# A conditioned residual kernel: convolution results of chunks 1 to 3 kept in DRAM, 29 adapter weights fetched ahead, D's row as an input

## The chip, the cores and the metric

The kernel runs on one core of a Trainium2 chip. The metric is the device time of one execution in microseconds (us); lower is better. Before the change it was run three times; the median is 2402.39 us (2400.78 to 2402.60). The trace that is shown comes from one more execution, taken by the hardware profiler.

The names of the engines are those of the profile: PE is TensorE (PEld its weight load), DVE is VectorE, ACT is ScalarE, POOL is GpSimd, and SP is SyncE, which here only issues DMAs. "SPq" in the trace is the queue of SP. Every engine carries out its own list of instructions in the order of the list.

## The reference

The input x has 32 sequences of 64 rows and 1024 columns, all float32. Four layers are added to it one after the other, each with indices per sequence:

```python
x = x + L0(x, log_dt, C, log_A_real, A_imag, D, length)   # long convolution
x = x + einsum('bsi,boi->bso', x, w1[ids1])               # first adapter, 1024x1024 per sequence
x = x + einsum('bij,bkj->bik', x, w2[ids2])               # second adapter
x = x + L3(x, W_gate, W_up, W_down, low-rank parts)       # gated layer, 2752 hidden columns

def L0(u, ...):
    K = 2 * real(einsum('hn,hnl->hl', Ct, exp(P)))        # one filter of 1024 taps per row h
    y = causal_convolution(u, K) + u * D[:, None]
    return y * (arange(1024) < length[:, None])[:, None, :]
```

Since D multiplies u itself, it may be added to the first tap of the filter of its row.

## The kernel before

The 32 sequences are four chunks of eight (`NCK`, `BC`). A chunk is a tile x of 128 partitions x 8 x 512 float32 (2 MB): the 1024 columns are 8 tiles (`KT`) of 128 partitions, and the 512 columns of a tile are 8 sequences x 64 rows. Only two such tiles have a permanent place (`xpool`, two buffers).

**Convolution** (`convolution`, lines 600 to 883). It runs over the rows h of all sequences at once. `kernels(g)` builds the filters of a group of 4 or 8 rows from sines, cosines and exponentials (POOL for the arguments, line 698, then DVE and ACT), multiplies them on PE into `pk` (line 804) and writes them through ACT's queue to DRAM (`kp`, line 816). D enters as a product of its own: POOL writes D's values of the group into an otherwise zero tile `dk` (line 778), which PE multiplies by a selecting matrix (line 795, 32x256). `convolve` (line 823) then takes four rows: it loads the input `uf` (512 KB) and, from `kp`, for two rows at a time, the shifted filters `hk` (1 MB, line 833), runs 16 products for each pair (line 845), masks the result on DVE into `tmp`, and POOL adds `tmp` to the x tiles of all four chunks, four instructions of 128x256 (line 861). All four x tiles therefore have to be on chip: two in `xpool` and two in `x2pool`. 16 calls of `convolve` cover the 64 rows.

**Adapters** (`adapter`, line 163; `adapters`, line 199). For one sequence and one of the two adapters eight weight tiles of 512 KB are loaded by SP, chosen by an index which SP reads from `ids_sb`, and PE multiplies them (line 184, 64 products). DVE transposes the result and adds it to x (lines 195 and 197). A weight goes into one of nine places `early`, or, once these are used up, into one of the nine buffers of `wpool`, which all weights of the kernel share. All 16 calls of chunk 0 (128 weight tiles, 64 MB) run right after the convolution, and `early` is released after them.

**Gated layer** (`ffn`, line 458), once for each chunk: `rest` (line 401), products of 128x512 with three weights `wr`, and in it `expand` (line 297) with the gathered rows `bgu` of the low-rank part; then ten blocks `gated(c, m)` (line 346), each of which starts with `expand(b_rows(c, m), ...)`: POOL gathers 128 rows by an indirect DMA (line 221) into the single buffer of `bgu`, and PE multiplies them (line 305) before the big products `pf` (line 361). After each half of a block `between` is called, which interleaves the adapters of the next chunk (`other`). `prepare` computes the low-rank columns of the next chunk. POOL also issues the loads of the columns `raw_g`, `raw_u`, `raw_d` (line 249); the buffer of `raw` is single, so that the next set waits for ACT's copy (line 254).

**x of chunks 2 and 3**. In the first `between` of chunk 0, POOL writes both tiles to DRAM (`park`, line 126), and at the first `between` of chunks 1 and 2 SP loads one of them back (line 485) into the buffer of `xpool` that the chunk before has left, after its output has been written (line 589, ACT's queue).

**Order.** PE's list is the order of the program text (`manual_schedule(engines={PE})`). The lists of the other engines are drawn up by a scheduler from its own estimate of times; `issue_after` gives it an earliest place. The DMAs that SP and ACT issue use eight completion semaphores in turn; a DMA waits for the one that used its semaphore before.

Of the kernel before, what the change touches and what calls it, by code (L numbers as in the profile page):

```python
# [8 lines left out]
F32 = mybir.dt.float32  # L9
I32 = mybir.dt.int32  # L10
AF = mybir.ActivationFunctionType
ALU = mybir.AluOpType
# [17 lines left out]
EARLY = 9  # L30
# [35 lines left out]
def kernel(  # L66
# [44 lines left out]
    def x_tile(pool, c, tag):  # L111
        return pool.tile([P, KT, TC], F32, tag=tag, name=f"x{c}")

    ctx.enter_context(tc.manual_schedule(engines={PE}))
    xs = [x_tile(xpool, c, "x") for c in range(2)]

    right = ExitStack()
    x2pool = right.enter_context(tc.tile_pool(name="x2pool", bufs=1, side="right"))
    first = right.enter_context(ExitStack())
    epool = first.enter_context(tc.tile_pool(name="epool", bufs=1, side="right"))  # L120
    late = [x_tile(x2pool, c, f"x{c}") for c in range(2, NCK)]
    early = [epool.tile([P, L], F32, tag=f"e{i}", name=f"early{i}") for i in range(EARLY)]
    blocks = convolution(tc, cst, consts, xt, xf, ssm, lens, xs + late, ps_tile)
    parked = []

    def park():
        for c, x_c in enumerate(late, 2):
            d = dpool.tile([P, KT, TC], F32, tag=f"xd{c}", name=f"xd{c}")
            nc.gpsimd.dma_start(d, x_c)
            parked.append(d)  # L130

    ids_sb = cpool.tile([1, 3 * B], I32, tag="ids", name="ids_sb")
    nc.sync.dma_start(ids_sb, ids)

# [25 lines left out]
    loads = []  # L160
    ypool = ctx.enter_context(tc.tile_pool(name="ypool", bufs=2, reuse_waits="tile"))

    def adapter(w, layer, b):
        c, lo = b // BC, (b % BC) * H
        with ExitStack() as after:
            if len(loads) > 3:

                after.enter_context(tc.issue_after(loads[-4]))
            e = nc.values_load(
                ids_sb[0:1, layer * B + b : layer * B + b + 1],  # L170
                engines=[SP],
                min_val=0,
                max_val=NE - 1,
            )
        acc = ps_tile(f"pa{layer}_{b}")
        for kt in range(KT):
            name = f"wa{layer}_{b}_{kt}"
            wt = early.pop(0) if early else wpool.tile([P, L], F32, tag="w", name=name)
            load = nc.sync.dma_start(
                wt, w[bass.ds(e, 1), kt].rearrange("e p f -> p (e f)")  # L180
            )
            for s in range(2):
                for i in range(4):
                    nc.tensor.matmul(  # L184
                        acc[i * S : (i + 1) * S, s * 256 : (s + 1) * 256],
                        xs[c][:, kt, lo + s * S : lo + (s + 1) * S],
                        wt[:, i * 256 : (i + 1) * 256],

                        start=(kt == 0 and s == 0),
                        stop=(kt == KT - 1),  # L190
                        skip_group_check=True,
                    )
        loads.append(load.ins)
        y = ypool.tile([P, 512], F32, tag="y", name=f"y{layer}_{b}")
        nc.vector.transpose(y, acc)  # L195
        cols = xs[c][:, :, lo : lo + H].rearrange("p k (s t) -> p k s t", t=S)
        nc.vector.tensor_add(cols, cols, y.rearrange("p (s k t) -> p k s t", s=2, t=S))

    def adapters(c):


        for b in range(c * BC, (c + 1) * BC + 1):
            if b < (c + 1) * BC:
                yield adapter(w1, 0, b)
            if b > c * BC:
                yield adapter(w2, 1, b - 1)

    with tc.issue_after(blocks[5]):

        pieces = adapters(0)  # L210
        for _ in range(3):
            next(pieces)
    for _ in pieces:
        pass
# [18 lines left out]
    apools = []  # L233
# [112 lines left out]
    def gated(c, m, xb, between):  # L346
# [47 lines left out]
        act = apools[0].tile([P, 2, TC], F32, tag="act", name=f"act_{c}_{m}")  # L394
# [63 lines left out]
    def ffn(c, xb, others):  # L458
# [6 lines left out]
        def other(share, of=2 * FM * AT_GATED + (2 * KH - 3) * AT_DOWN):  # L465
            due[0] += share * NPIECE
            while due[1] * of < due[0]:
                next(others, None)
                due[1] += 1

        def between(i):
            if i == 0 and c == 0:
                with tc.issue_after(cols[-1]):
                    park()
                right.close()
                apools.append(
                    ctx.enter_context(
                        tc.tile_pool(
                            name="apool", bufs=MB, side="right", reuse_waits="tile"
                        )  # L480
                    )
                )
            if i == 0 and c and c + 1 < NCK:
                x_n = x_tile(xpool, c + 1, "x")
                nc.sync.dma_start(x_n, parked[c - 1])
                xs.append(x_n)
            other(AT_GATED)
# [3 lines left out]
        for block, (m0, m1) in enumerate(BLOCKS):  # L491
# [7 lines left out]
            if last:  # L499


                wl = gpool.tile([P, 2, 2, L // 2], F32, tag="wl", name=f"wl_{c}", bufs=1)
                for t in (0, 1):
                    wl_t = wl[:, t].rearrange("p i f -> p (i f)")
                    gather(wl_t[FIRST], bd, rows_half[FIRST, c, t : t + 1])
                    nc.sync.dma_start(wl_t[SECOND], wd_rest)
                nc.vector.tensor_sub(wl[:, 1, 0], wl[:, 1, 0], wl[:, 1, 1])
            else:
                ins += [rest1, rest2.rearrange("p i t -> p (i t)")]

            ab = []
            for i, act in enumerate(acts):
                t3 = apools[0].tile([P, 4, TH], F32, tag="actd", name=f"actd_{c}_{m0 + i}")
                q = [act[:, h, t * TH : (t + 1) * TH] for h in (0, 1) for t in (0, 1)]
                ab.append(moving(*q, *(t3[:, j] for j in range(4))))
# [84 lines left out]
def convolution(tc, cst, consts, xt, xf, ssm, lens, xs, ps_tile):  # L600
# [9 lines left out]
    with ExitStack() as ctx:  # L610
# [12 lines left out]
        for c in range(NCK):  # L623
            nc.sync.dma_start(xs[c], xt[:, c])
# [141 lines left out]
        zero = s1.tile([HG, P], F32, tag="zero", name="zero")  # L766
        nc.vector.memset(zero, 0.0)


        dk = s1.tile([P, HG, LQ], F32, tag="dk", name="dk")  # L770
        nc.gpsimd.memset(dk, 0.0)

        def kernels(g):
# [3 lines left out]
            r = powers(g, y, s1, "r")  # L777
            nc.gpsimd.tensor_copy(dk[0:1, :n, 0], dskip[0:1, h0 : h0 + n])
# [15 lines left out]
            ps = ps_tile(f"pk{g}")[:LQ, : n * LQ]  # L794
            nc.tensor.matmul(
                ps,
                cst[:, CO_SEL : CO_SEL + LQ],
                dk[:, :n].rearrange("p h l -> p (h l)"),
                start=True,
                stop=False,  # L800
                skip_group_check=True,
            )
            for i in range(n):
                nc.tensor.matmul(
                    ps[:, i * LQ : (i + 1) * LQ],
                    gt[:, i, :],
                    et[:, i, :],
                    start=False,
                    stop=True,
                    skip_group_check=True,  # L810
                )
            ks = s2.tile([LQ, HG, LQ], F32, tag="ks", name=f"ks{g}")
            nc.scalar.copy(ks[:, :n].rearrange("a h b -> a (h b)"), ps)
            kp = dram.tile([n, KROW], F32, tag=f"kp{g}", name=f"kp{g}")
            nc.scalar.dma_start(kp[:, :P], zero[:n])
# [5 lines left out]
        loads = []  # L821

        def convolve(kp, row, ha):

            uf = s3.tile([P, 4, KT, B], F32, tag="uf", name=f"uf{ha}", bufs=2)
            nc.sync.dma_start(uf, xf[:, ha : ha + 4])
            tmp = s2.tile([P, 4, KT * B], F32, tag="tmp", name=f"tmp{ha}")
            for i in range(0, 4, 2):
                hk = s3.tile([P, 2, L], F32, tag="hk", name=f"hk{ha + i}")

                for j in range(0, 2, 1 if ha == 0 else 2):
                    n = 1 if ha == 0 else 2
                    load = nc.sync.dma_start(
                        hk[:, j : j + n],
                        bass.AP(
                            tensor=kp.tensor,
                            offset=kp[row + i + j : row + i + j + 1, 1:2].offset,
                            ap=[[1, P], [KROW, n], [1, L]],
                        ),
                    )  # L840
                loads.append(load.ins)
# [16 lines left out]
            tv = tmp.rearrange("p i (k b) -> p k b i", b=B)  # L858
            for c in range(NCK):
                xv = xs[c].rearrange("p k (b h) -> p k b h", h=H)[:, :, :, ha : ha + 4]  # L860
                nc.gpsimd.tensor_tensor(xv, xv, tv[:, :, c * BC : (c + 1) * BC, :], ALU.add)
# [15 lines left out]
        for g, n in enumerate(GROUPS):  # L877
            h0 = sum(GROUPS[:g])
            for i in range(0, n, 4):
                convolve(ready[g], i, h0 + i)  # L880
                if i == 0 and g + 2 < len(GROUPS):
                    ready.append(kernels(g + 2))
        return loads
# [19 lines left out]
def _layouts(np, v):  # L903
# [8 lines left out]
    def states(a):  # L912
# [10 lines left out]
            np.broadcast_to(v["L0_cond_D"], (P, H)),  # L923
# [4 lines left out]
    def adapters(w):  # L928
        w = w.reshape(NE, KT, 4, S, KT, P)
        return w.transpose(0, 4, 5, 2, 1, 3).reshape(NE, KT, P, L)  # L930
# [104 lines left out]
```

## Time and profile before

| | us |
|---|---|
| median of three runs | 2402.39 |
| the profiled execution | 2400.47 |
| its span, first to last instruction | 2398.80 |
| PE busy | 2324.7 (97% of the span) |
| POOL busy | 206.8 (9%) |
| DMA, mean over the span | 209 GB/s |

Three stretches can be told apart. From 0 to some 196 us the filters are built and the convolution runs. From 197 to 360 us PE runs the adapters of chunk 0 and waits again and again for a weight; the DMA engines are full there. From then on the gated layers follow, in which PE is busy nearly all the time: of the stretch from 440 to 2000 us the table of stages shows every microsecond as busy. A wait that is added to PE's list there has nothing beside it that could hide it, and where PE is busy all the time a wait of another engine costs nothing.

In the lines of the timeline the first number is the start in us, the second the length, then engine, line of the kernel, operation, output and inputs, the shape, the number of instructions that are merged, and in brackets how long the engine was idle before and what ended that.

### The profile page before, as it was taken

The numbers are of one execution on the slowest core, as the hardware profiler recorded it, in microseconds if no ns is written. First come the engines' busy times: TensorE is split into PE (matmuls) and PEld (weight loads), VectorE is DVE, ScalarE is ACT, GpSimd is POOL, SyncE is SP. The second block draws the span as 40 slices with busy tenths as digits, with TensorE's granted clock in tenths as the row PEclk, the third lists the DMA queues.
The fourth block names the chain that finished last, engine by engine and source line by source line (L and its number), as shares of the span: only waits on it lengthen the run. The fifth ranks groups of instructions, "written<-read, shape, count | busy, mean of one in ns | idle before, by whom it ended". The sixth has DMA issues, their size and how long they took to land.

```text
span 2398.8 us, 46172 instructions
## 1 busy us (share of the span) xinstructions
PE 2324.7 (97%) x19154; PEld 1837.2 (77%) x19154; DVE 1087.4 (45%) x2067; ACT 310.8 (13%) x605; POOL 206.8 (9%) x301
## 2 busy tenths in 40 slices
PE   4998888999999999999999999999999999999999
PEld 3995335787787786788787786788787787888888
DVE  7511113454344543554344533554444544554653
ACT  4200002110011101110011101110011101210210
POOL 3533001000000020000000020000000020000000
PEclk9999999999999999999999999999999999999999
DMA  7889997656656646656756646655756543223311
GB/s 274 286 290 369 408 408 273 217 211 210 228 202 226 226 149 213 228 202 211 244 189 244 208 148 215 242 189 201 269 182 248 185 158 115 82 84 108 99 55 62
DMA packets 163139, 501.21 MB, mean 209 GB/s; under 512 B 20018, under 2 KB 54130, under 8 KB 161906
## 3 DMA queue, kind: packets, MB, share of 16 engines
q1 hardware_dynamic: 146434, 461.78, 55.2%
q0 software_dynamic: 9568, 27.80, 3.6%
q10 hardware_dynamic: 6928, 8.69, 1.0%
q8 instruction: 151, 2.47, 0.4%
q14 instruction: 58, 0.48, 0.1%
HBM read 485.31 MB, written 12.88 MB: 208 GB/s over the span
## 4 chain that ended last, share of the span: by engine, by line
PE 90%; DMA 7%; DVE 1%; ACT 1%; issue 0%; POOL 0%; SPq 0%; ACTq 0%; DVEq 0%; POOLq 0%
PE pf L361 41%; PE po L558 20%; PE pa L184 15%; DMA wa<-in_w 6%; PE pc L845 5%; PE pr L421 3%; PE po L553 2%; PE pe L305 2%; PE pl_d L277 1%; PE pl_u L277 0%; PE pl_g L277 0%; DVE br L645 0%; DMA ln<-in_lens 0%; DMA hk<-kp 0%; DMA kp<-ks 0%
## 5 line engine op out<-in xcount | busy, mean ns | idle before, releaser
L361 PE MATMUL pf<-xd,wf 128*128 128x256 f32 x2560 | 607.2, 381 | 0.0
L361 PEld LDWEIGHTS pf<-xd,wf 128*128 128x128 f32 x2560 | 481.6, 190 | 75.4 <-issue 7.4
L184 PE MATMUL pa<-wa,x 128*32 128x256 f32 x8048 | 468.8, 382 | 28.0 <-DMA wa<-in_w 26.4
L361 PE MATMUL pf<-xd,s 128*128 128x256 f32 x1920 | 453.7, 379 | 2.3 <-ACT c L377 2.3
L184 PEld LDWEIGHTS pa<-wa,x 128*32 128x32 f32 x8048 | 248.2, 110 | 241.2 <-DMA wa<-in_w 70.5
L361 PEld LDWEIGHTS pf<-xd,s 128*128 128x128 f32 x1920 | 364.7, 190 | 52.3 <-ACT c L377 2.7
L845 PE MATMUL pc<-uf,hk 128*128 128x256 f32 (+7 forms) x1024 | 151.8, 311 | 11.8 <-DMA hk<-kp 11.8
L221 POOL DMA_INDIRECT bgu<-in_bgu,rows x44 | 45.5, 1033 | 1354.8 <-PE pe L305 1305.7
L558 PE MATMUL po<-act,wd 128*128 128x256 f32 x640 | 161.7, 383 | 0.0
L845 PEld LDWEIGHTS pc<-uf,hk 128*128 128x128 f32 x1024 | 147.3, 194 | 15.9 <-issue 12.0
L558 PE MATMUL po<-actd,wd 128*128 128x256 f32 x640 | 159.0, 379 | 0.0
L558 PE MATMUL po<-actd,s 128*128 128x256 f32 x640 | 159.0, 379 | 0.0
L386 DVE TENSOR_TENSOR c<-pf,u 128x256 f32<-128x256 f32 x80 | 34.0, 425 | 242.3 <-PE pf L361 242.3
L558 PEld LDWEIGHTS po<-act,wd 128*128 128x128 f32 x640 | 119.4, 190 | 22.9 <-issue 6.3
L558 PEld LDWEIGHTS po<-actd,wd 128*128 128x128 f32 x640 | 121.6, 190 | 16.5
L558 PEld LDWEIGHTS po<-actd,s 128*128 128x128 f32 x640 | 121.6, 190 | 16.5
L315 ACT COPY lt<-pe 128x512 f32<-128x512 f32 x160 | 82.2, 599 | 307.5 <-PE pe L305 216.1
L195 DVE STREAM_TRANSPOSE y<-pa 128x512 f32<-128x512 f32 x64 | 45.5, 711 | 142.0 <-PE pa L184 142.0
L390 DVE TENSOR_TENSOR c<-c,lt 128x1024 f32<-128x1024 f32 x80 | 98.0, 1225 | 6.4
L333 DVE TENSOR_TENSOR s<-wf 128x512 f32<-128x512 f32 x80 | 54.7, 684 | 89.3 <-DMA wf<-in_wg 43.3
L333 DVE TENSOR_TENSOR s<-wd 128x384 f32<-128x384 f32 x64 | 31.2, 487 | 129.7 <-PE po L558 95.8
L421 PE MATMUL pr<-x,wr 128*128 128x512 f32 x192 | 84.2, 595 | 0.0
(166 smaller groups left out, 1816.6 us busy)
## 6 DMA issues: line engine op xcount, KB each, us to landing
wa<-in_w SPq DMA_DIRECT2D x503, 512.0 KB
wf<-in_wg SPq DMA_DIRECT2D x80, 512.0 KB
wf<-in_wu SPq DMA_DIRECT2D x80, 512.0 KB
wd<-in_wd SPq DMA_DIRECT2D x96, 384.0 KB
hk<-kp SPq DMA_DIRECT2D x30, 1024.0 KB
x<-in_xt SPq DMA_DIRECT2D x4, 2048.0 KB
uf<-in_xf SPq DMA_DIRECT2D x16, 512.0 KB
wd<-in_wd SPq DMA_DIRECT2D x32, 256.0 KB
```

What stands on the lines that cost most here:

```text
L184: nc.tensor.matmul(acc[i * S : (i + 1) * S, s * 256 : (s + 1) * 256], xs[c][:, kt, lo + s * S : lo + (s + 1) * S], wt[:, i * 256 : (i + 1) ...
L195: nc.vector.transpose(y, acc)
L221: nc.gpsimd.indirect_dma_start(out=t, out_offset=None, in_=table, in_offset=bass.IndirectOffsetOnAxis(ap=at_, axis=0),)
L305: nc.tensor.matmul(ps[:, at_ * 2 * H : (at_ + 1) * 2 * H], bt[pair(j), g], tms[table][pair(j)], start=(g == 0), stop=True, skip_group_chec ...
L315: nc.scalar.copy(lt[:, :n, 2 * H * j : 2 * H * (j + 1)], ps[:, : n * 2 * H].rearrange("p (i t) -> p i t", i=n),)
L333: nc.vector.tensor_add(s1, a21, a22)
L361: nc.tensor.matmul(ps, ws[j][:, kt, :], xb[j][:, kt, :], start=start and kt == 0, stop=kt == KH - 1, skip_group_check=True,)
L390: nc.vector.tensor_add(cf, cf, lt[:, g].rearrange("p i t -> p (i t)"))
L421: nc.tensor.matmul(ps, wt[:, kt, :], xs[c][:, kt, :], start=(kt == 0), stop=(kt == KT - 1),)
L553: nc.tensor.matmul(pss[j], w, a, start=False, stop=False, skip_group_check=True)
L558: nc.tensor.matmul(pss[j], ws[j][:, i, :], ab[m - m0][j], start=(m == m0 and home[j] % 2 == 0), stop=(m == m1 - 1), skip_group_check=True,)
L845: nc.tensor.matmul(ps[:, j, d * B :], hk[:, j, d * P : (d + 1) * P], uf[:, i + j, : KT - d, :].rearrange("p k b -> p (k b)"), start=(d == ...
```

## The change

Six things change together.

1. **Chunks 1 to 3 wait in DRAM.** `convolve` adds `tmp` only to chunk 0 (one POOL instruction instead of four). The parts of the other three chunks are copied by POOL into a tile `co` (128x768) and written by POOL's queue to a DRAM tile `cd`: 16 writes of 384 KB, in pieces of 1 KB.
2. **x of chunks 1 to 3 is loaded when it is needed.** `bring(c + 1, part)` is called in the first two `between` of chunks 0 to 2. It loads x from the input (2 MB), loads the four quarters of the convolution's result (`cv`, 512 KB each, into buffers of `wpool`), and POOL adds them: 16 instructions of 128x256 for a chunk. `park` and the loads from it go.
3. **More weights ahead.** `early` has 16 places of its own and four more in the x tile which chunk 1 will use; with the nine of `wpool` 29 weights of the adapters can be fetched during the convolution. `fetch` asks for 14 in the first `convolve`, ahead of the first `hk`, and for one in each of the other 15.
4. **D's row.** D comes in as a row with zeros below it, and one product of 8 columns (4 in the small groups) adds it to the first column of each row of `pk`; `dk`, its copies on POOL and the product of 256 columns go. The zeros ahead of the filters are written once for all groups instead of nine times, and the arguments `r` of the filters get two buffers instead of one.
5. **The interleaving.** The first two `between` of a chunk bring x and do no adapter; the other calls share the 16 adapters, so that they come a little more densely.
6. **SP's list.** `ids_sb` is loaded first of all, since the early weights need the indices. The loads of `wd_rest` get an earliest place, after the loads of chunk 0's adapters.

The core of the diff:

```diff
-EARLY = 9
+EARLY = 16
+FIRST_LOADS = 14
+PLACES = EARLY + 4 + 9
+HA = 4
...
+    early += [
+        place[:, i : i + L // TC].rearrange("p k t -> p (k t)")
+        for i in range(0, KT, L // TC)
+    ]
+    cd = dpool.tile([NCK - 1, P, H // HA, HA * KT * BC], F32, tag="cd", name="cd")
...
+    def fetch(ha):
+        for _ in range(FIRST_LOADS if ha == 0 else 1):
+            if len(ahead) < PLACES:
+                ahead.append(next(stream))
+
+    convolution(tc, cst, consts, xt, xf, ssm, lens, xs[0], cd, ps_tile, fetch)
+
+    def bring(c, part):
+        if part == 0:
+            xs.append(x_tile(c))
+            with tc.issue_after(loads[2 * BC - 1]):
+                nc.sync.dma_start(xs[c], xt[:, c])
+        n = H // HA // 4
+        for q in (2 * part, 2 * part + 1):
+            t = wpool.tile([P, n, HA * KT * BC], F32, tag="w", name=f"cv{c}_{q}")
+            nc.sync.dma_start(t, cd[c - 1][:, q * n : (q + 1) * n])
+            for g in range(n):
+                h = (q * n + g) * HA
+                xv = xs[c].rearrange("p k (b h) -> p k b h", h=H)[:, :, :, h : h + HA]
+                tv = t[:, g].rearrange("p (i k b) -> p k b i", k=KT, b=BC)
+                nc.gpsimd.tensor_tensor(xv, xv, tv, ALU.add)
...
         def between(i):
-            if i == 0 and c == 0:
-                with tc.issue_after(cols[-1]):
-                    park()
...
-            if i == 0 and c and c + 1 < NCK:
-                x_n = x_tile(xpool, c + 1, "x")
-                nc.sync.dma_start(x_n, parked[c - 1])
-                xs.append(x_n)
-            other(AT_GATED)
+            if i < 2:
+                if c + 1 < NCK:
+                    bring(c + 1, i)
+            else:
+                other(AT_GATED)
...
-            r = powers(g, y, s1, "r")
-            nc.gpsimd.tensor_copy(dk[0:1, :n, 0], dskip[0:1, h0 : h0 + n])
+            r = powers(g, y, s2, "r")
...
             nc.tensor.matmul(
-                ps,
+                ps[:, :, 0],
                 cst[:, CO_SEL : CO_SEL + LQ],
-                dk[:, :n].rearrange("p h l -> p (h l)"),
-                start=True,
-                stop=False,
+                dskip[:, h0 : h0 + n],
+                start=False,
+                stop=True,
                 skip_group_check=True,
             )
...
             uf = s3.tile([P, HA, KT, B], F32, tag="uf", name=f"uf{ha}", bufs=2)
             nc.sync.dma_start(uf, xf[:, ha : ha + HA])
+            fetch(ha)
...
-            tv = tmp.rearrange("p i (k b) -> p k b i", b=B)
-            for c in range(NCK):
-                xv = xs[c].rearrange("p k (b h) -> p k b h", h=H)[:, :, :, ha : ha + 4]
-                nc.gpsimd.tensor_tensor(xv, xv, tv[:, :, c * BC : (c + 1) * BC, :], ALU.add)
+            xv = x0.rearrange("p k (b h) -> p k b h", h=H)[:, :, :, ha : ha + HA]
+            tv = tmp.rearrange("p i (k b) -> p k b i", b=B)[:, :, :BC, :]
+            nc.gpsimd.tensor_tensor(xv, xv, tv, ALU.add)
+            co = s1.tile([P, NCK - 1, HA * KT, BC], F32, tag="co", name=f"co{ha}")
+            tv = tmp.rearrange("p i (k c b) -> p c (i k) b", k=KT, b=BC)[:, 1:]
+            nc.gpsimd.tensor_copy(co, tv)
+            nc.gpsimd.dma_start(
+                cd.rearrange("c p g e -> p c g e")[:, :, ha // HA],
+                co.rearrange("p c i b -> p c (i b)"),
+            )
```

The lists of the changed kernel's instructions, engine by engine, are known before it runs. Where they matter for the prediction, it says what stands in them.

## The prediction

> **What bounds the kernel now.** I read the page first: PE is busy for 97% of the span and the chain of waits is 90% PE, 7% DMA, with one DMA group that matters, the adapter weights.
>
> ```profile
> PE 90%; DMA 7%; DVE 1%; ACT 1%; issue 0%; POOL 0%; SPq 0%; ACTq 0%; DVEq 0%; POOLq 0%
> ```
>
> Then the table of stages, to see where these 7% lie (columns: window, length, busy us and instructions of each engine, granted clock, DMA share, GB/s):
>
> ```profile
> 120.00:180.00 60.00, 60.00 (x438) 58.13 (x437) 8.68 (x13) 0.72 (x2) 21.71 (x28) 1.00 0.85 290
> 240.00:300.00 60.00, 49.61 (x748) 19.87 (x744) 8.45 (x12) 1.99 (x2) 0.00 (x0) 1.00 1.03 408
> 420.00:480.00 60.00, 60.00 (x542) 47.34 (x545) 28.97 (x49) 8.59 (x19) 2.21 (x2) 1.00 0.61 216
> ```
>
> The convolution (first row) is bound by PE, with the DMA at 290 GB/s; the adapters of chunk 0 (second row) by the DMA at its limit of 408 GB/s; the gated layers (third row) by PE alone. In the first and third kind of stage a stall of PE is paid in full.
>
> Third, the timelines of PE, POOL and SP at the start of chunk 1, the place where the change puts new work:
>
> ```profile
> 905.86 0.52 POOL L433 MEMSET rest<- 64x512 f32 x1 [7.34 <-DVE x L581]
> 906.67 0.94 POOL L221 DMA_INDIRECT wl<-in_bd,rows_half  x1 [0.28 <-issue]
> 907.92 0.92 POOL L221 DMA_INDIRECT wl<-in_bd,rows_half  x1 [0.30 <-issue]
> 921.83 0.97 POOL L221 DMA_INDIRECT bgu<-in_bgu,rows  x1 [13.00 <-PE pe_rest L305]
> 930.00 0.96 POOL L221 DMA_INDIRECT bgu<-in_bgu,rows  x1 [7.20 <-PE pe L305]
> ```
>
> ```profile
> 905.85 1.16 SPq L506 DMA_DIRECT2D wl<-in_wd_rest  x2
> 917.30 0.34 SPq L485 DMA_DIRECT2D x<-xd  x1
> ```
>
> ```profile
> 921.38 7.13 PE L421 MATMUL pr<-x,wr 128*128 128x512 f32 x16
> 928.45 0.73 PE L305 MATMUL pe<-tm_g,bgu 32*128 32x128 f32 x16
> ```
>
> The gather of `bgu` for the first block is issued at 921.83, as soon as PE has released its buffer, and PE uses it at 928.45 without idling: 6.6 us of cover, no more. x of the next chunk is issued by SP only at 917.30, because it waits for the output of chunk 0. Before, nothing waits for that x for a long time. Last, the price of POOL's addition:
>
> ```profile
> 187.19 3.24 POOL L861 TENSOR_TENSOR x<-x,tmp 128x256 f32<-128x256 f32 x4 [5.96 <-DVE tmp L637]
> ```
>
> 0.81 us each undisturbed; the mean of 60 between 60 and 200 us is 0.89.
>
> **What the Trainium skill says.** "TensorE: Matmul & The Clock Gate", in its opening table, gives GpSimd a queue of strict order; the trace agrees (the gathers above run one by one in list order). "GPSIMD Engine Reference", section 3.1, measures about 2.6 cycles per element for a two-input addition; at 256 elements and 1.2 GHz that is an estimate of 0.55 us plus dispatch, below the trace's 0.81, which I use. "TensorE: Matmul & The Clock Gate", part 1, says that PE falls to half clock after an idle window of some 3.4 us and needs about as long to recover; the trace agrees: after the idle time from 54.7 to 59.1 us the clock of the window from 59 to 66 is 0.76, a loss of 0.24 x 7 = 1.7 us. "DMA: Bandwidth & Descriptors", section "Issuing engines are not separate DMA queues", says that queues share the same engines, so the new writes on POOL's queue take bandwidth from `hk`; no stage of this trace has both at full load.
>
> **The change, part by part.**
>
> *Adapters of chunk 0: -22.8 us.* Before, from the first product (197.27) to the last transpose (360.05), 162.8 us. PE takes a tile in 0.44 us (17 tiles in 7.55), the DMA delivers one in 1.28 (ten-odd pieces of 10.1 us for eight). After, 29 tiles lie ready, but SP's list continues with the 30th only when the first `wpool` tile, the 21st, has been used: 21 x 0.44 = 9.4 us, then some 1.5 us until data flow, then 99 x 1.28 = 126.5, then 1.3 for the last tile and 1.1 for its products: 140. If the gap is filled less well, 145; if the low-rank loads, now in the gap, leave the stream free, 136.
>
> *Convolution: about +1.3 us.* D's product costs 0.55 of PE in the steady part, six times on the path; the small one some 0.1: -2.7. On ACT's list the copy of the third group's filters now stands behind the sine argument of the group after next, where before it was released at 50.9; with `r` in two buffers the groups run closer (POOL's 1.5 us between groups go), so I take 2 us later, range 0 to 5. The 14 early weights are 7.3 MB ahead of the first `hk`, but 6 MB of x go from there. In the steady part one `convolve` (9.2 to 9.8 us) has to move 2.1 MB of `hk`, 0.5 `uf`, 0.5 weight, 0.4 writes = 3.5 MB, 9 us at 400 GB/s. That is barely hidden: I take +2, and +10 if 350 GB/s is the limit. POOL's copy of 128x768 isn't in the trace: at most three additions, 2.4 us, at least one, 0.8; with the remaining addition and a DMA it fits into 9 us in which POOL before had 3.3 us of additions.
>
> *Start of chunks 1 and 2: +14 us each.* In POOL's list of the changed kernel the 16 additions of `bring` stand behind the two `wl` gathers and ahead of the gather of `bgu` for the first block. PE's list has `pe` of this block directly behind `pr`, with nothing to do instead. x is issued at about 917.3 as before (it still waits for the output), 2 MB at 400 GB/s plus start lands at 924. 16 x 0.85 = 13.6: 937.6. The third and fourth quarter come in time; the fourth takes the buffer of the first and can be issued at 927. Then the gather: issue to landing is 4.4 us in the median of the 44. PE goes on at 942 instead of 928.45, 13.6, rounded to 14. Bounds: 9, if x lands 4 us earlier and additions take 0.81; 18, if the gather lands in 8 us as it did once in chunk 0 (382.04 to 390.2).
>
> *Start of chunk 0: +13 us.* Here the list has: two `raw_d` loads that wait for ACT's copy (375.28 to 376.75 before, 16.7 us after the end of the adapters), four additions, two loads, four additions, four loads with their index reads (1.18 each), eight additions with three index reads (0.65 each), then the gather. From 16.7: two loads 1.5, additions 13.6, two loads 1.2, four 4.7, reads 2.0 = 39.7, landing 4.4 to 8: 44 to 48 after the adapters, where PE before started at 30.2. Some 15, less the 2.3 us that PE before lost just behind it waiting for ACT's copy `c`. Here x has long landed (its load follows the last weights); bounds 9 and 17.
>
> *Clock: +4.5*, three stalls at 1.5 (0 to 1.7 each).
>
> *Hidden edits.* 4 MB written and read back go, 12 MB are read instead, in a stage that moves 216 GB/s: nothing. The denser adapters are the same PE work; `wpool` loses four buffers for a while, but the weights behind them are needed 25 us later: nothing, at worst 2.
>
> Sum: -22.8 + 1.3 + 28 + 13 + 4.5 = +24. On the profiled execution 2400.5 + 24 = 2424.5, which was 1.9 below the median of the runs; I take 2425.
>
> **Rivals.**
>
> *The gather isn't late (faster).* If POOL finishes the additions while PE is still in `pr`, only the gain is left: 2400.5 - 21.5 = 2379. For it: POOL is busy 9% of the time, and the additions are 13.6 us against 22 us of `pr`. Against: x can't land before the output of the old chunk is written, and PE frees `bgu` at 921.8. It decides from the point where the additions end by 924, that is, x landed by 910, before chunk 0's last output was even under way (906.8) for long. In chunk 0 the waiting `raw_d` loads are against it.
>
> *Half of it.* If x comes 7 us earlier or the additions take 0.5 us, the stalls are 6 to 7 us each: -21.5 + 20 + 4.5 = +3, 2404.
>
> *The convolution becomes DMA-bound.* Then 8 to 10 us come on top: 2434. For it: 3.5 MB in 9.2 us is 385 GB/s; against: in the trace single stretches reach 420.
>
> **How the numbers follow.** Forecast (late gathers, convolution hidden or nearly) 0.68, own range 2410 to 2436; with a DMA-bound convolution 0.10; half of it 0.12; gather not late 0.10. The range of 8 in 10 is 2404 to 2440. No change here means within 0.2% or 4.8 us, about what this measurement can tell. Slower 0.80, same 0.10, faster 0.10.
>
> **What would show it.** In the new profile: PE idle before `pe` for some 14 us, released by the DMA of `bgu`, three times and not in chunk 3; POOL's 16 additions directly ahead of the gather; the first adapter stage of about 140 us; granted clock below 1 just behind the stalls. The forecast is wrong if PE's idle time before `pe` is under 5 us, or if PE idles in the steady convolution.

## The result and the profile after

| | before | after |
|---|---|---|
| time, median of the runs | 2402.49 us | 2458.28 us |
| lowest to highest run | 2400.78 to 2405.94 | 2456.94 to 2459.07 |
| profiled span | 2398.8 us | 2455.3 us |
| mean granted clock of PE | 0.999 | 0.987 |

The changed kernel is slower by a ratio of 1.023, 95% interval 1.0212 to 1.0247: 56 us, where the forecast said 23 (its sum of parts, 24). Both medians are those of four runs. Five marks that both kernels have cut the span into stages: the first adapter product that waits for POOL's last addition to x, the last transpose of the adapters of chunk 0, and the first product `pr` of chunks 1, 2 and 3.

| stage | before, us | after, us | difference | forecast |
|---|---|---|---|---|
| convolution | 197.27 | 207.62 | +10.35 | +1.3 |
| adapters of chunk 0 | 162.78 | 154.33 | -8.45 | -22.8 |
| chunk 0 | 546.40 | 556.54 | +10.1 | +13 and clock 1.5 |
| chunk 1 | 535.64 | 556.52 | +20.9 | +14 and clock 1.5 |
| chunk 2 | 535.64 | 559.20 | +23.6 | +14 and clock 1.5 |

Chunk 3 takes the same time in both. The waits of PE in the kernel after (engine, line, what it waited for: us in total, times, longest us) name what is new:

```profile
PE pe L342 <- DMA bgu<-in_bgu,rows: 51.7, 3, 20.4
PE pa L230 <- DMA wa<-in_w: 22.8, 85, 1.5
PE pc L867 <- DMA hk<-kp: 13.5, 8, 8.9
```

The first line was 1.5 us in one wait before. It names a DMA, but the DMA is only the last link. The timeline of POOL at the start of chunk 1 after (start, length, engine, line, operation, in brackets the idle time before it and what ended that) shows what came ahead of it:

```profile
935.25 18.27 POOL L194 TENSOR_TENSOR x<-x,cv 128x256 f32<-128x256 f32 x16 [14.06 <-DMA x<-in_xt]
953.68 0.97 POOL L256 DMA_INDIRECT bgu<-in_bgu,rows  x1 [0.16 <-issue]
```

and that of PE:

```profile
933.41 7.13 PE L458 MATMUL pr<-x,wr 128*128 128x512 f32 x16
959.34 1.24 PE L342 MATMUL pe<-tm_g,bgu 32*128 32x128 f32 x16 [18.79 <-DMA bgu<-in_bgu,rows]
```

The gather leaves 0.16 us after the 16th addition, and PE starts 5.7 us after it, having stood for 18.8. The 16 additions take 1.14 us each here, not the 0.81 that one took before. The timeline of VectorE in the same place of chunk 2 shows why:

```profile
1493.49 0.69 DVE L450 TENSOR_TENSOR rest<-rest,cr 128x512 f32<-128x512 f32 x1
1494.10 1.33 DVE L371 TENSOR_TENSOR s<-s,wf 128x512 f32<-128x512 f32 x1
1499.10 0.68 DVE L467 TENSOR_TENSOR cr<-pr,lt_rest 128x512 f32<-128x512 f32 x1
```

These are three operations of one shape. The first starts 0.01 us before POOL's first addition (1493.50) and keeps its 0.69 us, while that addition takes 1.38. The second has to take turns with the additions and takes 1.33 us. The third runs beside them too, but one of its operands, `pr`, is a result of PE in PSUM, and it takes 0.68. Both engines are slowed while both read two operands from SBUF.

The chain of waits is of little use here:

```profile
PE 38%; DMA 1%; POOL 0%; DVE 0%; issue 0%; DVEq 0%
```

Its shares add up to 39%, that is, some 950 us: followed back from the end it breaks off at chunk 2's additions, and all before is missing. A chain that doesn't add up to 100% shows where it was lost, not that the rest is harmless.

The table of stages after (window, length, busy us of PE, PEld, DVE, ACT and POOL with instructions, granted clock, DMA share, GB/s):

```profile
120.00:180.00 60.00, 56.81 (x417) 55.04 (x416) 8.31 (x12) 0.72 (x2) 14.28 (x18) 1.00 0.97 353
180.00:240.00 60.00, 55.09 (x723) 41.38 (x725) 10.73 (x20) 1.04 (x1) 19.20 (x29) 1.00 0.63 217
210.00:225.00 15.00, 15.00 (x284) 9.06 (x280) 2.82 (x4) 1.04 (x1) 8.90 (x15) 1.00 0.36 114
225.00:240.00 15.00, 12.61 (x228) 6.96 (x224) 2.82 (x4) 0.00 (x0) 2.54 (x4) 1.00 0.92 307
```

In the steady convolution the DMA is at a share of 0.97 with 353 GB/s and PE no longer busy throughout. At the start of the adapters, where the transfers were to be the bound, they run at 114 GB/s until 225 us. The waits of SP's list between 186 and 262 us and its timeline say why:

```profile
SPq L160 <- PE pa L230: 33.8, 10, 31.1
```

```profile
225.59 35.69 SPq L160 DMA_DIRECT2D wa<-in_w  x30
```

SP stands for 31 us until PE frees the first buffer that may be loaded again, 20 us after the first adapter product.

### The profile page after: what moved, and what is told of

Same layout as the page of the kernel before. It is cut to its first block, busy times and chain, and to the rows that moved or that the text cites. A ratio compares the mean times of both kernels' runs of the same rounds, so it can differ in the third digit from the quotient of the medians.

```text
span 2455.3 us, 46187 instructions
## 1 busy us (share of the span) xinstructions
PE 2324.9 (95%) x19154; PEld 1840.9 (75%) x19154; DVE 1106.8 (45%) x2066; ACT 311.2 (13%) x605; POOL 242.1 (10%) x323
## 5 line engine op out<-in xcount | busy, mean ns | idle before, releaser
L230 PE MATMUL pa<-wa,x 128*32 128x256 f32 x7872 | 454.8, 381 | 24.1 <-DMA wa<-in_w 22.8
L230 PEld LDWEIGHTS pa<-wa,x 128*32 128x32 f32 x7872 | 242.0, 110 | 229.5 <-DMA wa<-in_w 60.7
L867 PE MATMUL pc<-uf,hk 128*128 128x256 f32 (+7 forms) x1024 | 153.4, 312 | 22.5 <-DMA hk<-kp 13.5
L867 PEld LDWEIGHTS pc<-uf,hk 128*128 128x128 f32 x1024 | 148.5, 195 | 27.1 <-issue 20.4
```

The source lines that it names most:

```text
L230: nc.tensor.matmul(acc[i * S : (i + 1) * S, s * 256 : (s + 1) * 256], xs[c][:, kt, lo + s * S : lo + (s + 1) * S], wt[:, i * 256 : (i + 1) ...
L867: nc.tensor.matmul(ps[:, j, d * B :], hk[:, j, d * P : (d + 1) * P], uf[:, i + j, : KT - d, :].rearrange("p k b -> p (k b)"), start=(d == ...
```

## The experiments

Stage times in this section are between the same marks, except that the first adapter product is taken as the first of all (195.51 us before, 205.86 after); the stage of the adapters is then 164.5 before and 156.1 after. Stage times and waits are those of the profiled execution. Where no ratio stands beside a time, it is that of a single run, and differences of a few us in it alone say little.

**The gather put first.** Additions are held back until the last gather of `bgu` has been issued:

```
+        gathered.append(got.ins)
...
+                with tc.issue_after(gathered[-1]):
+                    nc.gpsimd.tensor_tensor(xv, xv, tv, ALU.add)
```

> The kernel after, with one order changed: the 16 additions of chunks 2, 3 and 4 on POOL are issued after the gather of bgu that stood behind them; nothing is left out. If the stall is made by that gather's place in POOL's list, the three long PE waits on bgu (51.7 us in all) fall to a few us each and the time goes from 2458 to 2402-2412. If the late landing of x and of the parked results, the buffers that they hold, or the price of the additions themselves (1.14 us each beside DVE) makes the stall, the waits move to the weights or to the next gather and the time stays above 2440.

Measured: 2424.46 us, ratio to before 1.0105 (1.0088 to 1.0122). The long waits on `bgu` are gone, 3.4 us in one wait are left, and the clock is back at 0.996: the place in the list made the long stalls. But the time lies between the two expectations: of the 52 us, 34 came back by the medians (38 by the profiled executions; this one, at 2419.01, is below its median). Chunks 1 and 2 take 542.2 and 542.3 us, 6.6 more than before. POOL and PE in this kernel:

```profile
927.12 0.97 POOL L259 DMA_INDIRECT bgu<-in_bgu,rows  x1 [12.68 <-PE pe_rest L346]
928.37 18.41 POOL L197 TENSOR_TENSOR x<-x,cv 128x256 f32<-128x256 f32 x16 [0.28 <-DMA x<-in_xt]
```

```profile
941.52 2.00 PE L402 MATMUL pf<-xd,s 128*128 128x256 f32 x8 [1.23 <-ACT c L418]
948.18 3.04 PE L402 MATMUL pf<-xd,s 128*128 128x256 f32 x8 [2.94 <-DVE c L423]
```

The gather goes out as soon as PE frees its buffer. Now the additions cover the first half tile of the gated layer, where VectorE stands directly behind PE with its work for `rest` and the weights. PE waits twice: 1.2 us for a copy on ACT, whose list had itself stood 7.8 us for VectorE (4.9 before), and 2.9 us for VectorE. These are 4.2 of the 6.6 us.

**The additions left out**, all else as in the kernel after:

```
-                nc.gpsimd.tensor_tensor(xv, xv, tv, ALU.add)
```

> The kernel after with its order unchanged, but the 48 additions on POOL left out: the parked results of chunks 1 to 3 are written and loaded as before and not added, so chunks 1 to 3 are computed without their convolution. With the gather put first, a chunk still took 542.2 us against 535.6 before. If POOL's additions slow VectorE's on the same stretch, and so the first gated tile, chunks 1 and 2 go back to 535-537 each and the time is 2402-2407. If it is the load of x and of the parked tiles, or the buffers that they take, each chunk stays at 540 or more and the time at 2418 or more.

Measured: 2416.81 us, chunks 539.3 and 539.9. This is between the two expectations, because the run brought a wait of its own. VectorE's timeline:

```profile
936.47 0.69 DVE L529 TENSOR_TENSOR wl<-wl 128x512 f32<-128x512 f32 x1 [20.96 <-DMA wl<-in_wd_rest]
```

In this kernel SP's list has the loads of `wl` partly behind that of x, which waits for a buffer, and VectorE's list has this subtraction ahead of everything for the next tile. The run doesn't price the additions in chunks 1 and 2. It shows something of chunk 0, though: there PE still waits 7.8 us for the gather, with no addition ahead of it. The gather leaves 28.6 us after the last transpose of the adapters (22.0 before, 37.0 in the kernel after), behind eight loads of `raw_d` that follow ACT's copy; before, one stood there.

**The additions spread** over the first four half tiles, one parked quarter each, with the gather ahead of them as above. Adapters begin two half tiles later:

```
-            if i < 2:
+            if i < 4:
...
```

> The kernel after, with the gather ahead of the additions and the additions spread over four half tiles of the gated layers, four at a time, in place of two; nothing left out. If the slowing of VectorE costs time only where 16 additions stand without a gap in the first gated tile, a chunk falls from 542.2 us to 536-538 and the time to 2407-2414. If the sum of the additions counts wherever they stand, the chunks stay at 541-543 and the time near 2424. If the rotation of buffers that paces them is late, it is above 2424.

Measured: 2416.45 us, chunks 540.4 and 542.0. The chunks lie between the two expectations. Little is won, since eight of the additions still fell into the first half tile, where PE waited for VectorE for 3.1 us in chunk 1.

**The additions later**, in the third to sixth half tile, with x and the parked quarters loaded then, and again with the gather ahead. The adapters begin in the seventh:

```
-            if i < 2:
+            if 2 <= i < 6:
...
```

> The kernel after, with the gather ahead of the additions, and the loads of x and of the parked results and their additions moved from the first two half tiles of the gated layers to the third to sixth, four additions in each; nothing left out. In the first half tile VectorE stands just behind PE, after that it has slack. If the remaining 5-7 us of a chunk are the slowing of VectorE in the first half tile, chunks 1 and 2 take 535-538 us (with the gather first: 542.2; spread from the first half tile: 540.4) and the time is 2406-2413. If the additions cost their share wherever they stand, the chunks stay at 540-542 and the time at 2416 or more.

Measured: 2415.41 us, above the expectation, with a first adapter product at 209.5, 5.4 us later than in the run with the gather first, though the convolution is the same in both programs; that hides what the later stages gain. Chunks 1 and 2 take 538.4 and 538.1: some 4 of the 6.6 us are gone. The additions are the same 16, so it is the place that cost these (the later adapters were not tested apart); 2.4 to 2.7 us of a chunk remain, among them waits of PE of 1.22 for VectorE and up to 0.78 us for ACT.

**Weights fetched ahead: 14 instead of 29.**

```
-PLACES = EARLY + 4 + 9
+PLACES = 14
```

> The kernel after, with 14 weights fetched ahead and none of the further 15 during the convolution; nothing is left out. If the convolution is longer because the filters, the inputs, the writes of the parked results and the weights together ask for more than some 350 GB/s, the first adapter product comes at 198-202 us instead of 207.6 and the waits on filters (13.5 us) fall to half or less; the adapters after it start with fewer tiles at hand, their stage is 150-162 us (now 154.3). If the later start of the third filter group or the added write traffic makes it longer, the first adapter product stays at 205-208.

Measured: 2449.74 us. The first adapter product comes at 200.10, 5.8 us earlier, and the waits on filters are down to two, 10.7 us. That is not half of the 13.5, as 9 us of both are the wait before the very first filter, but the waits in the steady part are gone but for one of 1.5 us. The table of stages of this kernel:

```profile
120.00:180.00 60.00, 59.99 (x446) 58.54 (x444) 8.30 (x12) 0.72 (x2) 14.28 (x18) 1.00 0.93 326
```

PE is full again, with a DMA share of 0.93 at 326 GB/s. Rate by share gives 350 GB/s for a full DMA here, and 364 in the kernel after (353 at 0.97): it depends on the mixture of filters, inputs, weights and writes. Six profiles with the convolution of the kernel after have the first adapter product between 204.2 and 207.3 us and one at 209.5; all those with less to transfer have it at 200.1 or earlier. The stage of the adapters took 155.9 us, as long as with 29 weights at hand.

**No parking**: copies, writes and loads of the results of chunks 1 to 3 and the additions left out.

```
-            nc.gpsimd.tensor_copy(co, tv)
-            nc.gpsimd.dma_start(
...
```

> The kernel after without the parking: the copies and writes of chunks 1 to 3, the loads of the parked tiles and the additions are left out, so chunks 1 to 3 are computed without their convolution; the 29 weights are still fetched. If the transfers bound the convolution, taking 6.3 MB of writes out of it shortens it like taking out 7.9 MB of weights did (5.8 us): the first adapter product comes at 199-202 us instead of 205.9. If POOL's copies or the write's own issue cost the time, it comes at 196 or earlier; if neither, at 205 or later. The chunks after it are 535-537 us as without additions.

Measured: 2399.69 us; first adapter product at 199.62, chunks 1 and 2 536.9 and 535.8. Taking 6.3 MB of writes out helps as much (6.2 us) as taking 7.9 MB of weights out (5.8), and either alone frees PE: the convolution is bound by the sum of the transfers. It isn't the copies, which all stand in the run with 14 weights. In both runs the third group still began at 63.4 to 63.6 us, as in the kernel after (63.74; before 59.13), so this part has another cause.

**D's row alone, in the kernel before.**

```
-            nc.gpsimd.tensor_copy(dk[0:1, :n, 0], dskip[0:1, h0 : h0 + n])
...
+                ps.rearrange("a (h b) -> a h b", b=LQ)[:, :, 0],
+                cst[:, CO_SEL : CO_SEL + LQ],
+                dskip[:, h0 : h0 + n],
```

> The kernel before, with D's row as an input and one product of it for each group in place of the copy into a zeroed tile and the 256-column product; nothing else. Both theories of the convolution have it save 0.4 us of PE for each group, and the time go down by 1 to 4 us (2398-2401). If the wait for filters hides it, there is no difference beyond 1 us.

Measured: 2401.47 us, against 2401.85 for the kernel before (median of seven runs). The first adapter product comes 2.6 us earlier (192.92), and the last transpose at 360.21 as before (360.05). The gain is real where it is made and is given back in the next stage, which waits for weights and whose transfers end when they end.

**The places of the weights exchanged**: the first nine in the pool of nine buffers, the other 20 in the places that are used once.

```
-                wt = early.pop(0) if early else wpool.tile([P, L], F32, tag="w", name=name)
+                late = taken[0] <= 9 or not early
+                wt = wpool.tile([P, L], F32, tag="w", name=name) if late else early.pop(0)
```

> The kernel after, with only the places of the first 29 adapter weights exchanged: the first nine of them lie in the pool of nine buffers, the other 20 in the places that are used once. If the adapters of chunk 0 gain little because the first buffer that can be loaded again comes free only with the 21st tile (18 us in), SP's loads resume within 2 us of the first adapter product, and the stage of the adapters falls from 154.3 us to 137-142; the time goes to 2440-2446. If the rate of the weights' loads in the whole stage or the order of SP's list sets it, the stage keeps 150 us or more.

Measured: 2452.63 us, and the stage 151.7, 4.4 less and not 15. The table of stages of this kernel:

```profile
210.00:225.00 15.00, 15.00 (x284) 9.05 (x280) 2.82 (x4) 1.05 (x1) 7.16 (x13) 1.00 0.99 377
225.00:240.00 15.00, 15.00 (x288) 8.97 (x276) 2.82 (x4) 0.00 (x0) 3.53 (x6) 1.00 0.62 172
```

SP does resume at once, at 207.6. After nine tiles it stops again for 16.9 us, from 215.7 to 232.6, because PE is now using up the 20 places that nothing is loaded into. The hole has moved, not gone.

**One ring of 29**: each place is loaded again after use.

```
+                i = (taken[0] - 1) % 29
+                if taken[0] > (2 * BC) * KT or i < 9:
+                    wt = wpool.tile([P, L], F32, tag="w", name=name)
+                elif i < 9 + EARLY:
+                    wt = early[i - 9] if taken[0] <= 29 else epool.tile(...)
```

> The kernel after, with the 29 places of the adapters' weights used as one ring in chunk 0: each is loaded again once its product is done, not used once; nothing left out. Exchanging the places alone made the stage 151.7 us (after: 156.1, from the first adapter product to the last transpose), since the transfers stopped again for 12 us in the middle of the 20 places used once. If the hole in the transfers is all that stands against the gain, SP loads without a stop from 208 us, 99 tiles at 1.285 us each, and the stage is 137-141 us, the time 2439-2443. If something else in the list of SP or the rate of PE holds the stage, it keeps 148 us or more.

Measured: 2444.86 us, and the stage 139.5, inside the expectation: the hole was what stood against the gain. The time is 2 us above the expectation, since chunk 0 grew from 556.5 to 560.5 us, with a new wait of 11.2 us before `pl_u`.

**All together**: the gather first, the additions later and the ring, by the edits above, with 19 weights fetched ahead (`PLACES = 19`).

> All of it together, nothing left out: the gather ahead of the additions, the additions in the third to sixth half tile, the 29 places used as a ring (the stage of the adapters was 139.5 us with it), and 19 weights fetched ahead instead of 29 (with 14 the first adapter product came at 200.1 us). If the four causes are independent, the first adapter product comes at 201-204 us, the last adapter transpose at 342-347, chunks 1 and 2 take 535-538 us, and the time is 2387-2395, below the 2402 of the kernel before. If the gains stand in each other's place, the transfers that no longer run in the convolution make the adapters later by as much, and the time is 2398 or more.

Measured: 2405.74 us, ratio 1.0016 (1.0008 to 1.0024). The first adapter product came at 199.98 and the last transpose at 341.08, both better than expected, and chunks 1 and 2 took 538.7 and 538.3. The gains did not stand in each other's place, but chunk 0 took 565.2 us. PE's timeline of this kernel:

```profile
363.18 3.64 PE L326 MATMUL pl_u<-x,at_u 128*32 128x128 f32 x64 [15.39 <-ACT at_u L303]
```

In the kernel after, the loads of `raw_u` behind this wait went out from 221.7 to 228 us, early in the adapters; here from 344.85.

**The ring ended early**, with the 58th weight, all else as in the run before:

```
-                if taken[0] > (2 * BC) * KT or i < 9:
+                if taken[0] > 58 or i < 9:
```

> As the run before with all of it together, but the ring of 29 places ends with the 58th weight; the last 70 of chunk 0 go through the pool of nine. In the run before, chunk 0 took 565.2 us (550.7 with the same additions and no ring), with a stall of 15.4 us before pl_u: its loads came only after the last weight. If that is because the buffers of the gated layers lie where the ring lies and come free with its last place, chunk 0 falls to 548-552, the stage of the adapters stays at 140-145, and the time is 2388-2394, below the 2402 of the kernel before. If it is the order of POOL's list, or the transfers that are still busy, the stall stays and the time is 2402 or more.

Measured: 2396.36 us, ratio 0.9977 (0.9969 to 0.9985), 2 us above what was expected. The wait before `pl_u` is back at 1.2 us, chunk 0 at 551.6, the stage of the adapters 146.2: 5 us given up for 14 gained. The buffers of the gated layers lie where the ring lay, and must come free in time.

**ACT's copy of the filters first**, on top of the run before. What was left is the third group. ACT's timeline in the kernel after:

```profile
54.83 0.63 ACT L678 ACTIVATE bk<-br 128x512 f32<-128x512 f32 x1 [4.92 <-DVE br L673]
55.36 0.35 ACT L838 COPY ks<-pk 32x256 f32<-32x256 f32 x1
```

PE had finished the product of the third group at 46.0 us; the copy stands behind an activation of the sixth group, which waits for VectorE.

```
+                if g >= 2:
+                    after.enter_context(tc.issue_after(copied[g - 2]))
                 cosine(co, r, k)
...
+            copied.append(nc.scalar.copy(ks[:, :n], ps).ins)
```

> As the run before (everything together, the ring ending with the 58th weight), with one order more: on ACT the copy of a filter group's product is issued ahead of the first activation of the group two later. In the kernel after, the copy of the third group stood 9 us behind its product, in back of an activation that waited 4.9 us for VectorE, and the third group of the convolution began at 63.7 us instead of 59.1 (57.1 with D's row alone). If that place in ACT's list is what makes it late, the third group begins at 56-58.5 us, the first adapter product comes at 192-196 us instead of 199.4, and of that 1 to 5 us reach the end: 2391-2395. If the filters' landing beside the 14 weights is what it waits for, it stays at 62 or later and the time at 2396.

Measured: 2389.17 us, ratio 0.9945 (0.9931 to 0.9958). The copy in this kernel, and what now stands behind it, the activation of the fifth group:

```profile
47.30 0.34 ACT L855 COPY ks<-pk 32x256 f32<-32x256 f32 x1
47.55 0.62 ACT L690 ACTIVATE bk<-br 128x512 f32<-128x512 f32 x1
```

The copy is 8 us earlier, the third group 4.2 us: it begins at 59.46 (1 us later than expected; 57.13 with D's row alone), and what holds it there is open. The first adapter product comes at 195.3, and the gain reaches the end: the profiled span is 2390.0 us, 4.7 less than in the run before. The medians differ by 7.2, which the profiles don't explain in full. This version has all parts of the change, with 19 weights ahead instead of 29, and is 0.55% faster than the kernel before and 2.8% faster than the changed one (2389.17 of 2458.28).

## Why the prediction was right in direction and wrong in size

Of the 32 us between the forecast sum of +24 and the measured +56, the stage of the adapters makes 14.4, the convolution 9.0 and chunks 1 and 2 together 13.5; chunk 0 came 4.4 below its forecast.

- **Adapters, -22.8**: this is the largest miss, and the step that failed is "PE takes a tile in 0.44 us (17 tiles in 7.55)". The line that was read, with the one ahead of it, shows the nine early tiles of the kernel before:

```profile
195.51 0.64 PE L184 MATMUL pa<-early,x 128*32 128x256 f32 x8
197.27 7.55 PE L184 MATMUL pa<-early,x 128*32 128x256 f32 x136 [1.12 <-POOL x L861]
```

These are 144 records, 16 for a tile and not 8, so that the second line holds 8.5 tiles and one takes 0.88 us. The 21st tile is therefore used 18 us after the start, not 9.4, and the transfers stop for twice as long. With 18.0 in its place the forecast's own sum gives 148.4 us; 154.3 were measured. Part of the other 6 may be the slow restart (307 GB/s between 225 and 240 us instead of 408); this was not tested apart. The price of a tile's transfer, 1.28 us, fits: in the run with one ring the DMA moves 407 to 408 GB/s from 240 to 345 us. But that this run took 139.5 us, where the forecast had 140, is luck. The 140 contain a hole of 9.4 us, which that run doesn't have; from the mark that the forecast used (the product that waits for POOL) it took 137.8, and the forecast's sum without the hole would be 131, again some 6 us less than measured.

- **Late gathers at chunks 1 and 2**: right in mechanism and place; putting the gather first removed these stalls. Mis-sized were two terms. The addition was taken from the convolution at 0.81 to 0.89 us, but it is 1.14 us in chunk 1 beside VectorE: 18.3 us for 16 instead of 13.6. And the gather takes 5.7 to 6.0 us until PE runs instead of 4.4. In chunk 1 these are 4.7 + 1.3, less 0.8 since the additions began that much earlier behind `pr` than forecast: the stall grows from 13.6 to 18.8 us, as measured. In chunk 2 the additions (17.8) make 4.2, the gather 1.6 and a later start 0.9: 20.3, where 20.4 were measured.
- **Late gather at chunk 0**: the stall of 12.5 us, of 15 forecast, is near in sum and less so in its parts. The additions took 13.9 us, as forecast, but the eight loads among them with their index reads took 4.4 instead of 9.4, and the list came to them 2 us later. That the additions weren't dearer here is not for want of work on VectorE. It was VectorE that stood, 6.56 us in one addition, while seven of POOL's last eight ran through:

```profile
391.54 6.56 DVE L450 TENSOR_TENSOR rest<-rest,cr 128x512 f32<-128x512 f32 x1
391.92 6.87 POOL L194 TENSOR_TENSOR x<-x,cv 128x256 f32<-128x256 f32 x8
```

The additions aren't all of this stall either. Of the 15 us by which the gather left later than before, 6.6 remain without any addition, behind the loads of `raw_d`. Putting the gather first left a wait of 3.4 us here, and the last version still has 5.9. No run moved these loads.

- **Contention was not in the forecast at all.** The Trainium skill, "GPSIMD Engine Reference", section 1 (Specifications), says that GpSimd's SBUF interfaces are shared with VectorE, with contention where a VectorE instruction has two SBUF inputs; "SBUF — State Buffer", section "SBUF: two separate sides", calls it an exclusive lock. The trace agrees in kind. Of 24 such operations of 128x512 that ran beside POOL's additions, 20 took 1.12 to 1.33 us instead of 0.69, and an addition took 1.28 (the median of 48) instead of 0.82: where the two engines take turns, each pair takes some 1.3 us where the two alone would add up to 1.5. In chunk 0 seven of POOL's additions ran without giving VectorE a turn.
- **Convolution, +1.3**: two terms were too small. The delay of the third group was foreseen at 2 us, range 0 to 5. It is 6.6 against the kernel before with D's row alone (63.74 and 57.13); the copy's place on ACT was worth 4.2 of them, the rest is open. The transfers were put at +2, with 10 "if 350 GB/s is the limit"; the runs with fewer weights or no writes put their cost at 5.8 and 6.2. The gain from D's row is 2.6 us at its place, as forecast (2.7). Together that is 9.8 to 10.2 of the 10.35 measured. In the kernel before, the gain from D's row isn't one of the whole: the stage behind it takes it back.
- **Clock, +4.5**: the order of size is right. What chunks 0 to 2 grew beyond PE's idle time is 1.5, 2.1 and 2.9 us; the granted clock is 0.76, 0.74 and 0.61 in the 6.6 to 7 us behind the stalls, the first `pf` product after the stall in chunk 2 took 3.49 us instead of 1.99, and the mean clock rises from 0.987 to 0.996 when the long stalls go. (The idle time from which the forecast took its price was 3.4 us, from 55.8; at 54.7 PE still had products of a filter group.)
- **Rivals.** A DMA-bound convolution was given 0.10 and is what happened beside the late gathers; the forecast's own sign of being wrong, that PE idles in the steady convolution, came true (56.81 us busy of 60). The other two, with the gather in time or half so, were wrong. The range failed because errors were taken as small and independent; the term for PE's time per tile was a plain misreading, worth 8.6 us by itself.

## What to carry to other kernels

Before pricing a buffer scheme, count the records that belong to one use of a buffer, and ask when the first reusable buffer comes free: places used only once hide a start and leave a hole of the same length behind it. Work moved onto an idle engine has two prices, its own and that of the neighbour that it slows, and its place in a strictly ordered list can cost more than both. A gain made in front of a stage that waits for transfers was lost here as long as the transfers ended when they had ended before (D's row alone).

## What was not expected of the hardware

- POOL and VectorE, both adding two SBUF operands, run in steps of some 1.3 us instead of 0.82 and 0.69, or one of them stands for several instructions of the other (6.56 us).
- The DMA's full share stands for different rates: 408 GB/s for 512 KB weight tiles, some 350 to 364 for the convolution's mixture of filters, inputs, weights and small-row writes.
- Spread over later half tiles, the same 16 additions cost 2.4 to 2.7 us in a chunk instead of 6.6.
